# Layer 2's outer rows written from PSUM straight to interleaved columns, with inner and outer rows in output tiles of their own

## The chip, the cores and the metric

The kernel runs on one core of a Trainium2 chip. The metric is the time of one execution on the device, in microseconds (us). Before the change three runs took 1878.82, 1880.79 and 1884.20 us; the median is 1880.79. Engines are named as in the profile: PE is TensorE's matmul and PEld its weight load, DVE is VectorE, ACT is ScalarE, POOL is GpSimd and SP is SyncE. "L785" is line 785 of the kernel's file.

## The reference

Two layers of the same form work on x, which is (8 images, 32 channels, 252 x 252) in float32. Each layer normalizes its input by groups of two channels and adds a 5x5 convolution of that to it:

```python
def _gn(v, G=16, eps=1e-5):
    B_, C_, H_, W_ = v.shape
    g = v.reshape(B_, G, C_ // G, H_, W_)
    m = jnp.mean(g, axis=(2, 3, 4), keepdims=True)
    s = jnp.var(g, axis=(2, 3, 4), keepdims=True)
    return ((g - m) / jnp.sqrt(s + eps)).reshape(v.shape)
...
x = x + _L0_conv_ref(_gn(x), L0_conv_weight)
x = x + _L1_conv_ref(_gn(x), L1_conv_weight)
return x
```

The convolution pads by reflection (two pixels on each side) and is written with FFTs in the reference: `xp = jnp.pad(x, ..., mode='reflect')`, a product of transforms summed over the input channels, and the inverse transform without the border. Its output has the size of its input.

## The kernel before

**Layout.** A partition holds one channel of one of four phases: even or odd columns (`cp`) and even or odd rows (`rp`) of the image; `quad(cp, rp)` gives the 32 partitions of a phase, `halves[cp]` the 64 partitions of a column phase. On these phases the 5x5 convolution is a 3x3 convolution from 128 to 128 partitions. So a result tile has columns of one phase beside each other on a partition, and image rows need the two column phases interleaved again before they go out.

**Chunks.** An image is worked in 8 chunks of 16 phase rows (`NCH`, `ROWS`), a chunk as 4 tiles (`NT`) of 4 rows. Vertically a tile is computed by the polynomial method with six points: VectorE makes sums of input rows (`t24`, `t13`, `t05`), TensorE multiplies them with the weights of points 0 to 5, three column taps each (`product`, L685), and the products are put together. Rows 1 and 2 of each tile, the inner rows, need points 1 to 4 only. Rows 0 and 3, the outer rows, need point 0 and point 5 as well. In some chunks (`by_columns`) points 0 and 5 are treated by the same kind of method along the columns: VectorE makes sums and differences (`columns`, L618 to L628, into `sdiff` and `d`), TensorE multiplies four and four times at half length (`column_product`, L707, into `extra` and `sums`). The other chunks are called plain here.

**PSUM.** `m24` has points 2 and 4, `pairs13` points 1 and 3, `sums05` the two outer rows (bank e for row 0 or 3), `extra` the middle products of the column method. `sums05` is one tile for all chunks. VectorE writes into it what points 1 to 4 give to the outer rows (in plain chunks `parts05`, L763 and L764; in column chunks `column_parts`, L792 to L794), then TensorE adds the rest, then ScalarE reads it.

**Order.** All work stands in a table of due times, written by hand (`at`). The functions are called in the order of these times, and each engine executes its instructions in that order. A slot is 10.2 us long by the table, plus 5.1 us if the products of points 0 and 5 of a plain chunk stand in it, or 1.7 us for a column chunk. Chunks of layer 1 of image b+1 and of layer 2 of image b alternate (`order`); this document names a chunk by image, layer (0 for layer 1, 1 for layer 2) and number, as the code does: (3,1,4). For chunk i, `conv` is called with t0, t1 and t2, the starts of slots i, i+1 and i+2. In slot i are the products of points 1 to 4 and the inner rows. The products that complete the outer rows stand at the end of slot i+1. The outer rows are read at the start of slot i+2 (t2+0.05): by `outer` (L773, plain) or `outer_columns` (L785, columns), two ScalarE instructions each. They write into `y`, a tile of 16 rows.

**Layer 2's output.** In layer 2 `store` follows. `interleave` copies from y into an output tile `o` with every second column, for one of four groups of 4 rows and both column phases (L925): 8 copies of 64 partitions x 508 per chunk, at t2+0.7, +4.0, +6.5 and +8.5. An output tile holds 8 rows of the chunk (h is 0 or 1), and has buffers of its own pool, `opool`, of two. `send` issues the DMAs on SP's queue (L910), four per tile, at t2+5.3 and t2+9.8. The last chunk but one, (7,1,6), has its copies on VectorE and its DMAs on POOL's queue. In chunks (0,1,0) and (6,1,5) all is done in one slot (`m05`): there the outer rows come by VectorE (L771) from another tile. The last chunk, (7,1,7), is done in two halves (`store_half`).

**What stands around the read of sums05.** On ScalarE: before it the squares of layer 1 (L860) in some slots; after it two copies L925, then the seeds of `pairs13` (L729, L731), then the evacuation of `m24` (L737), `first_pair` (L744), and the seed of the middle products (L711). On VectorE: the write for the next chunk (L763 or L792) comes after points 0 and 5 (`points05`, L609) and before the sums of `columns`.

## Time and profile before

| | |
|---|---|
| three runs | 1878.82, 1880.79, 1884.20 us (median 1880.79) |
| the profiled execution | 1879.27 us, its span 1877.5 us |
| PE busy | 1839.2 us, 98% of the span |
| DVE busy | 1731.2 us, 92% |
| ACT busy | 1493.8 us, 80% |
| POOL busy | 396.2 us, 21% |
| ACT copies from y to o (L925) | 496 of 660 ns on average, 327.5 us |
| ACT reads of sums05 (L785, L773) | L785: 158, 94.5 us; L773 of 128x508: 45, 24.3 us |
| DMA | 369.07 MB, 197 GB/s on average |
| chain that ended last | 80% PE, 7% DVE, 6% DMA, 3% ACT |

How to read it: the span is the time from the first to the last instruction of the profiled execution, and the execution's own time is a little longer. A busy share is the time in which the engine had an instruction under way. A row of the groups gives line, engine, operation, output and input with their shapes, the number of instructions, then the busy time in us and the mean of one in ns, then the idle time of the engine just before them and what ended it. A row of the time line gives start and duration in us, and in brackets the idle time before it. A row of the waits gives the waiting instruction and whom it waited for, then us in total, the number of times and the longest. A row of the windows gives for a stretch of time the busy us of each engine with the number of instructions, then the granted clock of PE, the DMA share and GB/s.

### The profile page before, as it was taken

Reading aid. Unit: us, or ns where it says so; the run is one execution under the profiler, and the core shown is the slowest. Engines: PE = TensorE matmul, PEld = TensorE weight load, DVE = VectorE, ACT = ScalarE, POOL = GpSimd, SP = SyncE. Lnnn points to the kernel's source line nnn. Section 1 sums busy time; section 2 is a strip of 40 time slices with the busy share of each in tenths; the row PEclk is TensorE's granted clock in tenths of the full one; section 3 lists DMA queues with packets and bytes.
Section 4 is the critical chain, followed back from the end, with each engine's and each line's share of the span. In section 5 each row is a group of like instructions: output and inputs, shape, how many; then the busy total and the mean of one; then the engine's idle time right before and its main releaser. Section 6 shows DMA issues by size and latency. Waiting matters only on the chain.

```text
span 1877.5 us, 20381 instructions
## 1 busy us (share of the span) xinstructions
PE 1839.2 (98%) x5194; PEld 966.0 (51%) x5194; DVE 1731.2 (92%) x3030; ACT 1493.8 (80%) x2781; POOL 396.2 (21%) x855
## 2 busy tenths in 40 slices
PE   5999999999999999999999999999999999999998
PEld 4444455545555555555555455554555555555455
DVE  7988799999999999999999899999999999997796
ACT  5886788878887888888898798987898876765575
POOL 4543111131112211122111311113111141110211
PEclk8999999999999999999999999999999999999999
DMA  9877578878888877987878967888878866775785
GB/s 275 203 179 180 151 209 199 210 194 202 217 202 219 194 209 192 221 223 173 220 193 206 235 175 205 205 204 204 212 202 198 214 165 140 179 174 148 195 212 125
DMA packets 207110, 369.07 MB, mean 197 GB/s; under 512 B 19088, under 2 KB 173968, under 8 KB 196752
## 3 DMA queue, kind: packets, MB, share of 16 engines
q1 hardware_dynamic: 178832, 230.73, 49.8%
q0 software_dynamic: 27600, 134.20, 29.3%
q10 hardware_dynamic: 560, 2.83, 0.4%
q8 instruction: 41, 0.67, 0.2%
q14 instruction: 77, 0.63, 0.1%
HBM read 167.15 MB, written 67.39 MB: 125 GB/s over the span
## 4 chain that ended last, share of the span: by engine, by line
PE 80%; DVE 7%; DMA 6%; ACT 3%; issue 3%; SPq 0%; POOL 0%; DVEq 0%; ACTq 0%; POOLq 0%
PE m L685 28%; PE pairs L685 28%; PE sums L707 7%; PE extra L707 6%; PE sums L685 6%; PE extra L685 4%; DMA v<-y 2%; DMA st<-in_x_dram 1%; DMA v<-ytail 1%; DMA xs<-in_x_dram 1%; ACT o L925 1%; DVE sd L748 1%; DVE t L609 1%; DMA wraw<-in_L_conv_weight_dram 1%; DMA out_dram<-o 0%
## 5 line engine op out<-in xcount | busy, mean ns | idle before, releaser
L685 PE MATMUL pairs<-t,u 128*128 128x504 f32 (+2 forms) x1548 | 692.9, 586 | 5.4 <-ACT pairs L729 3.3
L685 PE MATMUL m<-t,u 128*128 128x508 f32 (+3 forms) x1560 | 674.8, 581 | 3.4 <-DVE u L526 1.9
L685 PEld LDWEIGHTS m<-t,u 128*128 128x128 f32 x1560 | 294.2, 189 | 317.1 <-issue 297.0
L685 PEld LDWEIGHTS pairs<-t,u 128*128 128x128 f32 x1548 | 290.2, 189 | 320.1 <-issue 289.1
L925 ACT COPY o<-y 64x508 f32<-64x508 f32 x496 | 327.5, 660 | 8.6
L748 DVE SCALAR_TENSOR_TENSOR sd<-sd,pairs 128x504 f32<-128x504 f32 (+2 forms) x258 | 164.2, 671 | 19.5 <-PE pairs L685 15.2
L707 PEld LDWEIGHTS extra<-sdiff,wc 128*128 128x128 f32 x680 | 125.9, 189 | 98.1 <-issue 47.8
L707 PE MATMUL extra<-sdiff,wc 128*128 128x252 f32 (+3 forms) x680 | 173.0, 376 | 3.4 <-ACT extra L711 2.3
L860 ACT ACTIVATE junk<-y,negk 128x1008 bf16<-128x1008 f32 (+1 forms) x144 | 147.4, 1024 | 31.1 <-PE extra L707 14.5
L557 POOL DMA_DIRECT2D v<-y x63 | 35.7, 567 | 622.7 <-DVE t L609 608.4
L737 ACT COPY sd<-m 128x504 f32<-128x504 f32 (+2 forms) x258 | 136.9, 581 | 33.3 <-DVE sums L794 28.1
L609 DVE SCALAR_TENSOR_TENSOR t<-v 128x1024 f32<-128x1024 f32 (+1 forms) x128 | 157.7, 1232 | 5.4 <-PE sums L685 5.4
L707 PE MATMUL sums<-d,u 128*128 128x252 f32 (+3 forms) x680 | 157.4, 374 | 0.0
L707 PEld LDWEIGHTS sums<-d,u 128*128 128x128 f32 x680 | 127.6, 189 | 24.9 <-issue 9.0
L685 PE MATMUL sums<-t,u 128*128 128x508 f32 (+5 forms) x312 | 133.6, 577 | 0.0
L567 DVE TENSOR_TENSOR v<-xs 128x1792 f32<-128x1792 f32 (+1 forms) x65 | 130.2, 2003 | 1.2
L241 ACT ACTIVATE st<-st,negk 128x1134 f32<-128x1134 f32 x98 | 121.7, 1242 | 3.2
L559 POOL DMA_DIRECT2D v<-y x63 | 54.3, 862 | 329.1 <-DMA v<-y 329.1
L159 ACT COPY xs<-xs 64x1792 f32<-64x1792 f32 (+2 forms) x97 | 109.3, 1129 | 13.4 <-POOL xs L151 11.1
L729 ACT ACTIVATE pairs<-m,means 128x504 f32<-128x504 f32 (+1 forms) x129 | 84.2, 653 | 44.5 <-PE m L685 36.0
L785 ACT ACTIVATE y<-sums 128x504 f32<-128x504 f32 (+1 forms) x158 | 94.5, 634 | 28.3 <-PE sums L707 19.2
L235 ACT ACTIVATE st<-st 128x1134 f32<-128x1134 f32 x98 | 112.5, 1148 | 5.0 <-DMA st<-in_x_dram 3.2
(174 smaller groups left out, 2529.7 us busy)
## 6 DMA issues: line engine op xcount, KB each, us to landing
v<-y POOLq DMA_DIRECT2D x63, 1032.0 KB, 6.1
st<-in_x_dram SPq DMA_DIRECT2D x111, 567.0 KB, 6.1
out_dram<-o SPq DMA_DIRECT2D x480, 126.0 KB, 5.9
v<-y POOLq DMA_DIRECT2D x63, 903.0 KB, 7.7
xs<-in_x_dram SPq DMA_DIRECT2D x96, 441.0 KB, 8.4
xs<-in_x_dram SPq DMA_DIRECT2D x44, 504.0 KB, 12.0
u<-ud SPq DMA_DIRECT2D x15, 1152.0 KB, 6.0
xs<-in_x_dram SPq DMA_DIRECT2D x16, 472.5 KB, 9.3
```

The lines of the kernel that those rows point to most:

```text
L159: copy(t[64:128, :, 0:256:2], t[0:64, :, 1:256:2])
L235: A.activation(junk, src, AF.Identity, accum_out=acc[:, 0, i : i + 1])
L241: A.activation(junk, src, AF.Square, bias=negk, accum_out=acc[:, 1, i : i + 1])
L567: (V.tensor_add if l else V.tensor_sub)(v[:, r0:r1], t[:, r0 + 2 : r1 + 2], t[:, r0:r1])
L609: stt(t, got["vt"][:, :, 0:2], 4.0 if l else -4.0, got["vt"][:, :, 2:4], ALU.mult, ALU.add)
L685: T.matmul(dst, u[:, k, 2 - i, :], rhs[:, j0 + i0 : j0 + i1, i : i + wo], start=(i == 0 and not add), stop=(i == 2), skip_group_check=add,)
L707: T.matmul(dst[:, 0, use], w, rhs[:, use], start=(i == 2), stop=True, skip_group_check=(i != 2))
L737: A.copy(got["sd"][:, 1 + e], m24[e][:, 0:n])
L748: stt(d, d, -2.0, pairs13[e][:, 0:n], ALU.mult, ALU.add)
L785: A.activation(y, src, AF.Copy, scale=1.0 - 2 * i, **total(3 * i))
L860: A.activation(dst, src, AF.Square, bias=negk, scale=1.0 if i else -1.0, accum_out=acc[:, 1, at_ : at_ + 1])
L925: copy(got["o", h][halves[s], 0:m, cp::2], got["y"][halves[cp], r : r + m, :])
```

## The change

In layer 2, chunks that are not done in one slot no longer copy their outer rows through y. `outer_out` reads a bank of sums05 on 64 partitions (one column phase) and writes it with every second column into an output tile: four instructions per chunk at t2+0.05, on ScalarE, where two on 128 partitions stood. For the column chunks the odd half of a bank now begins at column 256 of it (`half`), so that one instruction can read both halves; and the difference that was kept with the other sign is kept as it is (`columns`, `column_parts`), because a plain copy can't change a sign.

Output tiles now hold the outer rows (0 and 3 of all four tiles) or the inner rows (1 and 2), and not the first or second 8 rows. The inner rows are still copied from y, four copies per chunk at t2+4.0 and t2+6.5. The DMAs are again four per tile, now with every eighth image row; they stand at t2+3.3 for the outer tile and t2+9.8 for the inner one. An output tile is 256 columns wide, not 254.

For (7,1,6) the inner rows are copied by VectorE at t1+7.0, before the last outer products; of the outer rows row 0 is copied by ScalarE and row 3 by VectorE. The chunks (0,1,0) and (6,1,5) copy all from y as before, into the new tiles.

```diff
-                V.tensor_sub(d[:, :, :, 1, 0:mo], odd[:, :, :, 0:mo], t[:, :, :, 3 : 2 * mo + 2 : 2])
+                V.tensor_sub(d[:, :, :, 1, 0:mo], t[:, :, :, 3 : 2 * mo + 2 : 2], odd[:, :, :, 0:mo])
...
-            return tile_[:, e, i * nt * ne : i * nt * ne + nt * m].rearrange("p e (t w) -> p e t w", t=nt)
+            return tile_[:, e, i * nt * ne : (i + 1) * nt * ne].rearrange("p e (t w) -> p e t w", t=nt)[:, :, :, 0:m]
...
+        def outer_out(e: int, engines):
+
+            if e == 0:
+                got["outer"] = out_tile(b, c, "outer")
+            t = slice(*tiles(5 * e))
+            for cp, eng in enumerate(engines):
+                to, bank = got["outer"][halves[e]], sums05[halves[cp], e]
+                if columns:
+                    dst = to.rearrange("p t (j i a) -> p t i j a", i=2, a=2)[:, t, :, :, cp]
+                    src = bank[:, 0 : 2 * nt * ne].rearrange("p (i t j) -> p t i j", i=2, t=nt)[:, t]
+                else:
+                    dst, src = to[:, t, cp : 2 * wo : 2], rows(bank[:, 0:n])[:, t]
+                (eng.copy if eng is A else eng.tensor_copy)(dst, src)
...
-            V.tensor_sub(odd, m2[:, :, :, 0:no], odd)
-            V.tensor_sub(half(sums05, 1, both, no), odd, m12[:, :, :, 0:no])
+            if l:
+                V.tensor_sub(odd, odd, m2[:, :, :, 0:no])
+                V.tensor_add(half(sums05, 1, both, no), odd, m12[:, :, :, 0:no])
+            else:
+                V.tensor_sub(odd, m2[:, :, :, 0:no], odd)
+                V.tensor_sub(half(sums05, 1, both, no), odd, m12[:, :, :, 0:no])
...
-                at(t2 + 0.05, outer_columns, i)
+                if l == 0:
+                    at(t2 + 0.05, outer_columns, i)
+                else:
+                    at(t2 + 0.05, outer_out, i, (A, A))
...
-            at(t2 + 0.05, outer, 0)
-            at(t2 + 0.05, outer, 1)
+            for e in range(2):
+                if l == 0:
+                    at(t2 + 0.05, outer, e)
+                else:
+                    at(t2 + 0.05, outer_out, e, (V, V) if e and (b, c) == (B - 1, NCH - 2) else (A, A))
...
+    def out_tile(b: int, c: int, name: str):
+
+        pool, tag = (spool, "st") if last_but_one(b, c) else (opool, "o")
+        return pool.tile([P, NT, 2 * WOUT[1] + 2], F32, tag=tag, name=f"o_{name}_{b}_{c}")
+
+    def store(t1: float, t0: float, b: int, c: int, got, from_y: bool):
+
+        end = last_but_one(b, c)
+
+        def interleave(name: str, k: int):
+            if k == 0:
+                got[name] = out_tile(b, c, name)
+            i = 3 * k if name == "outer" else 1 + k
+            n = NT - 1 if (c, i) == (NCH - 1, 3) else NT
+            copy = V.tensor_copy if end else A.copy
             for cp in range(2):
-                copy(got["o", h][halves[s], 0:m, cp::2], got["y"][halves[cp], r : r + m, :])
...
+                copy(got[name][halves[k], 0:n, cp : 2 * WOUT[1] : 2], got["y"][halves[cp], i : 4 * n : 4, :])
+
+        def send(name: str):
+            for k in range(2):
+                for rp in range(2):
+                    r = 2 * (c * ROWS + (3 * k if name == "outer" else 1 + k)) - 1 + rp
+                    use = [j for j in range(NT) if 0 <= r + 8 * j < H]
+                    j, m, q = use[0], len(use), 2 * k + rp
+                    (G if end else S).dma_start(
+                        out[b, :, r + 8 * j : r + 8 * (j + m - 1) + 1 : 8, :],
+                        got[name][q * Q : (q + 1) * Q, j : j + m, 1 : 1 + W],
+                    )
+
+        if from_y:
+            for k, t in enumerate((0, 3.3)):
+                at(t0 + t, interleave, "outer", k)
+        for k, t in enumerate((t1 + 7.0, t1 + 7.2) if end else (t0 + 5.8, t0 + 7.8) if from_y else (t0 + 3.3, t0 + 5.8)):
+            at(t, interleave, "inner", k)
+        at(t0 + (4.6 if from_y else 2.6), send, "outer")
+        at(t1 + 7.3 if end else t0 + 9.1, send, "inner")
```

In the changed file `outer_out`'s copies are L778, those of the inner rows L958, the DMAs L966, and the write of column chunks into sums05 begins at L806.

## The prediction

> **What bounds the kernel now.** I read the page first (busy time, then the chain), then who TensorE waits for, then the time line of one pair of slots, then windows. Busy time and the windows:
>
> ```profile
> PE 1839.2 (98%) x5194; PEld 966.0 (51%) x5194; DVE 1731.2 (92%) x3030; ACT 1493.8 (80%) x2781; POOL 396.2 (21%) x855
> ```
> ```profile
> 890.00:964.00 74.00, 74.00 (x215) 40.50 (x214) 73.20 (x118) 66.28 (x117) 10.61 (x27) 1.00 0.84 207
> ```
>
> TensorE's matmuls follow each other without a hole, at the full granted clock, and in the 74 us from 890 to 964 VectorE is busy for 73.20 as well: two engines are full, ScalarE (66.28) is not. A change that relieves ScalarE is worth only the places where TensorE waits for ScalarE, and a wait put on VectorE is worth what of it gets through to TensorE. The table of TensorE's waits says how little there is to win:
>
> ```profile
> PE pairs L685 <- ACT pairs L729: 3.3, 4, 1.3
> PE extra L707 <- ACT extra L711: 2.3, 8, 0.8
> PE pairs L685 <- ACT pairs L731: 2.1, 1, 2.1
> ...
> PE extra L707 <- DVE sdiff L619: 0.5, 2, 0.3
> ```
>
> **The change, part by part. ScalarE's count.** Before, a layer-2 chunk has 2 copies PSUM to y (L773 or L785) and 8 copies y to o (L925). After, it has 4 from PSUM to o and 4 from y to o. For 61 chunks two instructions of about 0.66 us go: 61x2x0.66, some 80 us of ScalarE's 1493.8. Beside a full TensorE this is worth nothing by itself.
>
> **The wait that it adds.** The next chunk's first write into sums05 (L792, on VectorE; L806 after) waits for the last ScalarE read of that tile. That was two instructions on 128 partitions; it becomes four on 64, in the same place of ScalarE's order. What happens at that place, in the slot after a plain (not by_columns) layer-2 chunk has been closed:
>
> ```profile
> 888.36 1.23 DVE L609 SCALAR_TENSOR_TENSOR t<-v 128x1032 f32<-128x1032 f32 x1
> 888.59 1.08 ACT L773 ACTIVATE y<-sums 128x508 f32<-128x508 f32 x2 [2.13 <-PE sums L685]
> 889.70 1.34 ACT L925 COPY o<-y 64x508 f32<-64x508 f32 x2
> 889.70 0.69 DVE L792 TENSOR_TENSOR sums<-extra,sd 128x504 f32<-128x504 f32 x1
> ```
>
> ScalarE can't start before TensorE's last matmul (888.59), ends at 889.67, and VectorE starts at 889.70, 0.1 us later than it could. So whatever the four copies take over 1.08 us delays VectorE. Rows for a price:
>
> ```profile
> L925 ACT COPY o<-y 64x508 f32<-64x508 f32 x482 | 319.9, 664 | 8.4
> L773 ACT ACTIVATE y<-sums 128x508 f32<-128x508 f32 x45 | 24.3, 591 | 67.6 <-PE sums L685 67.6
> L785 ACT ACTIVATE y<-sums 128x512 f32<-128x512 f32 x38 | 24.0, 630 | 19.2 <-PE sums L707 19.2
> ```
>
> Two L773 take 1.08 us, so the second starts 0.49 after the first: 0.10 of overlap. Two L925 take 1.34: none. All of ScalarE's copies on 64 or 32 partitions in this trace follow each other without overlap (L867 on 32 partitions: four in 1.27 us at 0.308 each), so I take none. One copy: source and size of L773 (0.594), output stride of L785 (0.630): 0.61. Four with 0.01 between: 2.47 us. VectorE's write moves from 889.70 to 888.59+2.47+0.03 = 891.09: **1.37 us later** (ends kept for the range: as four L773 with overlap 3x0.49+0.594 = 2.06, so 0.98; as four L925 at 0.677 apart 2.70, so 1.60). *The Trainium skill ("ScalarE: Activation LUTs", section "What ACT_TABLE_LOAD costs") says that back-to-back activations overlap by about 93 ns; by that alone the four would take about 2.2 us, an estimate, and the sum below would be about 1.7 us lower. L925's 1.34 for two at 0.664 each speaks against it here.*
>
> **What is queued behind it on VectorE.** All of the next slots' work. From 889.70 to 964 VectorE waits for nobody (no row in its waits there), so the 1.37 us are not caught up. Who notices first:
>
> ```profile
> 963.93 0.68 DVE L619 TENSOR_TENSOR sdiff<-t 128x504 f32<-128x504 f32 x1
> ...
> 964.95 1.01 PE L707 MATMUL extra<-sdiff,wc 128*128 128x252 f32 x4
> ```
> ```profile
> 1079.54 0.68 DVE L619 TENSOR_TENSOR sdiff<-t 128x504 f32<-128x504 f32 x1
> ...
> 1080.27 1.01 PE L707 MATMUL extra<-sdiff,wc 128*128 128x189 f32 x4
> ```
>
> In the second, TensorE is late and starts 0.05 us after sdiff ends (1080.22). In the first it starts 0.34 after (964.61), so the margin is 0.29. It shrinks to this over five slots (chunk (b,0,2) 2.4, (b,0,3) 1.3, (b,0,4) 0.29), because VectorE has some 0.5 us more work per column slot than TensorE. So TensorE loses 1.37-0.29 = 1.08 us, 0.1 of it at (b,0,3) and the rest at (b,0,4). The same starting place and margin are found for images 1 to 6 (L792 at 439.35, 664.51, 889.70, 1115.64, 1341.19, 1566.85, each within 0.1 of L773's end; margins 0.27 to 0.29). **6 x 1.08 = +6.5 us** (ends 6x0.69 = 4.1 and 6x1.31 = 7.9).
>
> In the other slots VectorE mostly reaches the write later than the new end: after column chunks it comes 0.6 to 2.6 us behind ScalarE, and is itself 1.37 late where it is 0.6. After the second plain chunk of an image, (b,1,4), it comes 0.5 to 1.3 behind, so 0.1 to 0.9 is added, where the sdiff margins that follow are 1.1 to 1.9: nothing is lost. Image 0 has 1.9 to 2.8 there. The last image (from 1749) has holes of 1 to 2 us in VectorE's row every slot and sdiff margins of 2.9 and more: nothing.
>
> **What of it stays.** After the loss VectorE is still 0.29 behind its old place. At the end of an image TensorE stands for the mean's matmul (L346, 1043.32; its input ends at 1043.17), which comes that much later: 5 x 0.29 = 1.4 at most. In two of the five VectorE waited just before that for ScalarE (0.24 and 0.78 us), which now comes earlier. I take **+0.8** (0 to 1.4).
>
> **What ScalarE's relief gives.** Two L925 leave the queue in front of L711 in slot (b,1,7):
>
> ```profile
> 843.69 1.32 ACT L925 COPY o<-y 64x508 f32<-64x508 f32 x2
> ...
> 844.90 0.59 ACT L711 ACTIVATE extra<-extra 128x512 f32<-128x512 f32 x1
> ...
> 845.54 1.02 PE L707 MATMUL extra<-sdiff,wc 128*128 128x256 f32 x4 [0.23 <-ACT extra L711]
> ```
>
> TensorE's starts there are 0.4 us late five times and 0.9 once: 2.9 us. But one slot later, (b+1,0,0), sdiff arrives with no margin in four of six images (1080.27 above): what TensorE wins it waits there. I take **-0.4** (0 to -2.9).
>
> **The end.** Chunk (7,1,6) is copied by VectorE. Two of its eight copies stand in the last chunk's chain:
>
> ```profile
> 1867.50 0.33 DVE y L758
> ...
> 1867.86 0.42 DVE o L925
> ...
> 1868.29 0.43 DVE o L925
> ...
> 1868.74 0.42 DVE sd L763
> ```
>
> After, they run at about 1856, where VectorE stands idle (4.47 us before 1860.14). VectorE's last y comes 0.87 earlier (1869.15); ScalarE's four earlier copies end at 1869.58 instead of being waited past to 1870.06. **-0.5** (0 to -0.9). POOL's queue sends the inner tile some 3 us earlier, no one waits for it.
>
> **Edits at nothing.** The swapped operands (L628, L793, L794) are the same instructions; VectorE's order is unchanged. The odd half at column 256 makes 76 matmuls and 38 adds write 4x63 with a gap: the write of 252 takes 377 ns, of 256 379; at most 152 x 0.002 = 0.3 us, 0 taken. Output DMAs are the same 8 per chunk of rows of 1008 B, in the same order on SP; the first four are issued about 2 us earlier, behind ScalarE's outer copies. o's buffers are still written 13 us or more after the last send. Seeds (L729): four copies (2.47) stand before them where L773/L785 and two L925 (2.42 to 2.50) stood, and TensorE needs them 1.4 us later.
>
> **Sum.** 6.5+0.8-0.4-0.5 = **+6.4 us**. The profiled execution took 1879.27 (span 1877.5), 1.5 below the median of the runs, 1880.79. I add to the median: **1887.2**. Ends: 4.1+0-2.9-0.9 = +0.3 and 7.9+1.4 = +9.3.
>
> **Rivals.** (1) *Not slower: the wait does not reach TensorE.* It needs the four copies done within 1.08+0.29 = 1.37 us, 0.34 each, or VectorE's add waiting for half of them alone. Against it: no ScalarE copy of this size is under 0.49 apart, and L806 writes both banks at once. Then the relief and the end remain, -0.9 to -3.8: about 1879. (2) *Slower by more: the traffic.* The DMA share is 0.84 there, VectorE already waits 17.6 us for the accumulating loads (v<-y, 7 times, longest 3.5), and outputs now leave 2 us earlier, against them. Margins of TensorE to those loads are 2.7 us and more, which speaks against it; if seven waits grow by 1 us past that, +7 on top: 1894. (3) *Nothing happens*: both engines' changes are hidden, 1880.8; it needs what (1) needs, and goes with it.
>
> **How the numbers follow.** Forecast case 0.74, rival (1) with (3) 0.16, rival (2) 0.10. A measurement can tell about 0.3% (5.6 us) from no change. The forecast case reaches from +0.3 to +9.3 with 6.4 taken, so about 0.62 of it lies over +5.6; with rival (2) slower is 0.46+0.10 = 0.56. Faster needs all of the -3.8 and more: 0.02. The rest, 0.42, is the same. The range takes in rival (1)'s middle and the forecast's upper end with a part of rival (2): 1879 to 1891.5.
>
> **What would show it.** Right: in the slots at 439, 664, 890, 1115, 1341 and 1567 VectorE's first write to sums waits 1.4 us for the new ScalarE line, of which TensorE's wait for sdiff (L619) shows about 1 us per image, at (b,0,3) and (b,0,4); the copies follow each other every 0.62 us; L711 no longer holds TensorE; the last chunk's L758 is followed by L763 at once. Wrong: copies every 0.5 us (a third less loss); no wait for sdiff, which would mean that VectorE's lateness has an exit that I did not see; or waits on v<-y that were not there.

## The result, and the profile after the change

The changed kernel took **1912.46 us** (median of 4 runs, 1910.19 to 1912.64), the kernel before 1879.80 in the runs beside it (4 runs, 1875.82 to 1884.20): a ratio of **1.0170**, with a 95% interval of 1.0146 to 1.0195. It is slower by some 33 us. The prediction, 1887.2 (1879 to 1891.5), had the sign right and the size wrong by 25 us. The profiled execution of the changed kernel took 1912.64 us, its span 1910.9.

The lines that answer those shown of before, in the same order. First busy time, and the window of 74 us that starts at the same slot as the one shown of before (there 890 to 964, with PE 74.00 and DVE 73.20):

```profile
PE 1850.6 (97%) x5194; PEld 961.6 (50%) x5194; DVE 1736.1 (91%) x3028; ACT 1491.1 (78%) x2661; POOL 400.6 (21%) x855
```
```profile
905.50:979.50 74.00, 72.52 (x210) 39.14 (x209) 70.39 (x113) 64.96 (x108) 11.52 (x24) 1.00 0.80 202
```

ScalarE has 120 instructions fewer than before (2661, not 2781) and yet is busy for only 2.7 us less (1491.1, not 1493.8), where the prediction expected 80. TensorE now has holes (72.52 of 74), and VectorE, which was full, has larger ones (70.39). The group of the new copies tells why ScalarE won nothing. This is the table of groups with shapes kept apart; the figure after the bar is the sum in us, then the mean of one copy in ns:

```profile
L778 ACT COPY o_outer<-sums 64x512 f32<-64x512 f32 x140 | 152.9, 1092 | 22.8 <-PE sums L707 21.2
...
L778 ACT COPY o_outer<-sums 64x508 f32<-64x508 f32 x88 | 54.4, 618 | 79.9 <-PE sums L685 78.8
```

A plain chunk's copy (64x508) takes 0.618 us, as priced (0.61). A column chunk's copy (64x512), of nearly the same size, takes **1.092**. What that does in the slots, from the time line (start, duration). Slot (3,1,1) stands behind a plain chunk, slot (3,1,2) behind a column chunk:

```profile
903.58 1.23 DVE L609 SCALAR_TENSOR_TENSOR t<-v 128x1032 f32<-128x1032 f32 x1
904.14 2.51 ACT L778 COPY o_outer<-sums 64x508 f32<-64x508 f32 x4 [2.37 <-PE sums L685]
906.68 0.69 DVE L806 TENSOR_TENSOR sums<-extra,sd 128x504 f32<-128x504 f32 x1 [1.88 <-PE m L685]
```
```profile
931.79 4.40 ACT L778 COPY o_outer<-sums 64x512 f32<-64x512 f32 x4
936.22 0.66 ACT L729 ACTIVATE pairs<-m,means 128x508 f32<-128x508 f32 x1
936.23 0.69 DVE L806 TENSOR_TENSOR sums<-extra,sd 128x504 f32<-128x504 f32 x1 [1.22 <-ACT o_outer L778]
...
936.93 3.67 PE L685 MATMUL pairs<-t,u 128*128 128x508 f32 x8 [0.49 <-ACT pairs L729]
```
```profile
953.94 0.68 DVE L619 TENSOR_TENSOR sdiff<-t 128x504 f32<-128x504 f32 x1
...
954.67 1.12 PE L707 MATMUL extra<-sdiff,wc 128*128 128x252 f32 x4 [0.47 <-DVE sdiff L619]
```

Behind the plain chunk four copies take 2.51 us (priced at 2.47). Behind the column chunk they take 4.40. Two things wait for them. The seed L729, which ScalarE writes into `pairs` before TensorE adds to it, starts 4.43 us after the first copy, and TensorE waits for it. In the same slot before, it started 2.53 us after L785 and ended 1.3 us before TensorE's matmuls on `pairs`:

```profile
916.24 1.14 ACT L785 ACTIVATE y<-sums 128x512 f32<-128x512 f32 x2
...
918.77 0.66 ACT L729 ACTIVATE pairs<-m,means 128x508 f32<-128x508 f32 x1
...
920.72 3.57 PE L685 MATMUL pairs<-t,u 128*128 128x508 f32 x8
```

VectorE's write L806 waits too, and hands its lateness on to the next sdiff (L619), for which TensorE waits at 954.67. The table of waits sums it up (us in total, times, longest):

```profile
DVE sums L806 <- ACT o_outer L778: 27.4, 34, 2.2
...
PE pairs L685 <- ACT pairs L729: 18.1, 27, 3.0
...
PE extra L707 <- DVE sdiff L619: 6.6, 14, 0.5
```

Before, TensorE waited 3.3 us for L729 and 0.5 for sdiff. Slot by slot (first matmul of one slot to the first of the next), from slot (2,1,0) to (3,1,0): five slots behind a column chunk of layer 2 are 0.74 to 0.80 us longer than before, two slots of layer 1, (3,0,3) and (3,0,4), 0.74 each, (3,0,7) with the mean's matmuls 0.63; (2,1,7) is 0.5 shorter and (4,0,0) 0.25 longer. The sum is +5.7, and the image took 231.0 us instead of 225.2.

Two smaller places that the prediction named are as it said. L711 no longer holds TensorE in slot (b,1,7), and in the last chunk L763 follows L758 at once:

```profile
858.85 0.58 ACT L711 ACTIVATE extra<-extra 128x512 f32<-128x512 f32 x1
...
860.15 0.92 PE L707 MATMUL extra<-sdiff,wc 128*128 128x256 f32 x4
```
```profile
1904.08 0.41 DVE L758 SCALAR_TENSOR_TENSOR y<-sd 128x254 f32<-128x254 f32 x1
...
1904.40 0.42 DVE L763 TENSOR_TENSOR sd<-pairs,sd 128x254 f32<-128x254 f32 x1
```

### The profile page after: what moved, and what is told of

It is laid out like the page before. It is cut to its first block, busy times and chain, and to the rows that moved or that the text cites. A ratio compares the mean times of both kernels' runs of the same rounds, so it can differ in the third digit from the quotient of the medians.

```text
span 1910.9 us, 20250 instructions
## 1 busy us (share of the span) xinstructions
PE 1850.6 (97%) x5194; PEld 961.6 (50%) x5194; DVE 1736.1 (91%) x3028; ACT 1491.1 (78%) x2661; POOL 400.6 (21%) x855
## 4 chain that ended last, share of the span: by engine, by line
PE 63%; DVE 13%; ACT 12%; issue 5%; DMA 2%; ACTq 0%; SPq 0%; DVEq 0%; POOL 0%
PE pairs L685 24%; PE m L685 19%; PE sums L685 6%; ACT o_outer L778 6%; PE sums L707 5%; PE extra L707 5%; PE extra L685 4%; DVE sd L748 1%; DMA out_dram<-o_inner 1%; ACT pairs L729 1%; ACT st L235 1%; DVE d L622 1%; DVE t L602 1%; DMA out_dram<-o_outer 1%; ACT junk L884 1%
## 5 line engine op out<-in xcount | busy, mean ns | idle before, releaser
L685 PE MATMUL pairs<-t,u 128*128 128x504 f32 (+2 forms) x1548 | 696.6, 588 | 23.6 <-ACT pairs L729 18.1
L778 ACT COPY o_outer<-sums 64x512 f32<-64x512 f32 (+1 forms) x242 | 218.6, 903 | 102.9 <-PE sums L685 78.8
L958 ACT COPY o_inner<-y 64x508 f32<-64x508 f32 x248 | 165.4, 667 | 6.4 <-DMA out_dram<-o_inner 2.6
L148 POOL COPY xs<-xs 64x4 f32<-64x4 f32 (+3 forms) x113 | 51.3, 454 | 378.8 <-DMA xs<-in_x_dram 282.2
L729 ACT ACTIVATE pairs<-m,means 128x504 f32<-128x504 f32 (+1 forms) x129 | 84.2, 653 | 50.4 <-PE m L685 46.5
```

The costliest lines, as they stand in the source:

```text
L685: T.matmul(dst, u[:, k, 2 - i, :], rhs[:, j0 + i0 : j0 + i1, i : i + wo], start=(i == 0 and not add), stop=(i == 2), skip_group_check=add,)
L729: A.activation(dst, src, AF.Identity, bias=norm[b, l][1][:, 0:1])
L778: (eng.copy if eng is A else eng.tensor_copy)(dst, src)
L958: copy(got[name][halves[k], 0:n, cp : 2 * WOUT[1] : 2], got["y"][halves[cp], i : 4 * n : 4, :])
```

## The experiments

**Theories.** The two shapes of L778 differ in how they go through the output. In a plain chunk neighbouring elements land 2 elements apart, 8 bytes. In a column chunk the pattern is "t i j": all even-half columns of a row first, then all odd-half ones, so neighbours land 4 elements apart, 16 bytes. Theory A: this distance makes the copy 1.10 us, and the length of the copies is the whole loss. Rival C: it is the source (two halves of a bank) or the pattern of one dimension more. Rival D: the new output tiles, their DMAs of every eighth row or the earlier sends cost time. Theory E is about the way in which the copies cost: not through the late seed alone, but through VectorE's wait as well.

For each kernel three figures are compared: the median with its ratio to the kernel before, run on the same chip; the time per image in the profiled execution, from the first matmul of slot (1,1,0) to that of (6,1,0), divided by 5; and the end, from TensorE's last matmul to the end of the span.

| kernel | median us | ratio (95%) | per image us | end us |
|---|---|---|---|---|
| before | 1878.4 to 1880.0 | 1 | 225.5 | 8.8 |
| changed | 1912.46 | 1.0170 (1.0146 to 1.0195) | 231.0 | 5.5 |
| other order | 1879.95 | 1.0007 (0.9998 to 1.0017) | 226.3 | 5.5 |
| 8 bytes, plain source | 1878.69 | 1.0007 (0.9998 to 1.0017) | 226.3 | 5.6 |
| tiles only | 1876.82 | 0.9991 (0.9980 to 1.0003) | 225.6 | 5.5 |
| columns only, other order | 1879.42 | 1.0003 (0.9993 to 1.0013) | 226.4 | 5.6 |
| plain only | 1884.78 | 1.0037 (1.0022 to 1.0052) | 227.8 | 5.5 |
| changed, seed between | 1940.01 | 1.0313 (1.0297 to 1.0329) | 235.6 | 5.7 |
| chunks 5 to 7 only, other order | 1872.81 | 0.9968 (0.9957 to 0.9980) | 225.1 | 5.5 |
| before, end on SP | 1874.67 | 0.9981 (0.9969 to 0.9992) | 225.3 | 5.7 |

**1. The other order of the same copy.**

```diff
-                    dst = to.rearrange("p t (j i a) -> p t i j a", i=2, a=2)[:, t, :, :, cp]
-                    src = bank[:, 0 : 2 * nt * ne].rearrange("p (i t j) -> p t i j", i=2, t=nt)[:, t]
+                    dst = to.rearrange("p t (j i a) -> p t j i a", i=2, a=2)[:, t, :, :, cp]
+                    src = bank[:, 0 : 2 * nt * ne].rearrange("p (i t j) -> p t j i", i=2, t=nt)[:, t]
```

> The computation is unchanged: only the order of elements within one column-chunk copy of the outer rows (L778) is another, row, then column pair, then even/odd, so that consecutive elements land 8 bytes apart instead of 16, while the PSUM source now jumps between the two halves of its bank (1 KB apart) at every element. Theory A (the 16-byte output stride is what makes this copy 1.10 us instead of the 0.61 that was predicted): the copy falls to 0.62 us, four take 2.5 us instead of 4.4, TensorE's waits for the seed L729 fall from 18 us to 4 or so and the time to 1880 to 1892. Theory C (the order of the source, or a pattern of one dimension more, is what is slow): the copy stays at 1.1 us or gets slower, and the time is 1910 or more. If the copy falls and the time stays above 1900, neither is the cause of the time.

The group of the same copies in this kernel, and its table of waits:

```profile
L778 ACT COPY o_outer<-sums 64x512 f32<-64x512 f32 x140 | 87.7, 626 | 23.9 <-PE sums L707 22.3
```
```profile
PE extra L707 <- DVE sdiff L619: 4.8, 7, 0.7
...
PE pairs L685 <- ACT pairs L729: 3.2, 4, 1.3
DVE sums L806 <- ACT o_outer L778: 2.7, 5, 1.3
```

The copy fell from 1.092 to 0.626 us, ScalarE's busy time to 1429.4 us (64 below before), the wait for L729 to 3.2 and the time by some 31 us (the ratio from 1.0170 to 1.0007), to that of the kernel before. One order of two nested loops made the whole loss. Theory A holds; C's jumping source costs nothing.

**2. The same distance with the source as it was.**

```diff
-                    dst = to.rearrange("p t (j i a) -> p t i j a", i=2, a=2)[:, t, :, :, cp]
+                    dst = to.rearrange("p t (i j a) -> p t i j a", i=2, a=2)[:, t, :, :, cp]
```

> Leaves out the interleaving of even and odd columns: in column chunks the outer rows are copied in the order of the changed kernel's source (the even half, then the odd half of each row) to output elements 8 bytes apart, so the two halves of a row lie side by side in the output instead of interleaved. Source as in the changed kernel, output stride as in the plain chunks. Theory A: the copy takes 0.62 us and the time is that of the kernel with the other order within 4 us, 1880 to 1892. Theory C: the copy stays at 1.1 us, and the time at 1912. If this one falls to 0.62 and the other order does not, then the jumping source is slow as well.

626 ns again, and the same ratio. So it is the output, not the source.

**3. The tiles and the DMAs alone.** Column chunks go back to `outer_columns` (with scale 1 for both halves in layer 2), plain ones to `outer`, and the outer tile is filled from y. Only (7,1,6) stays direct.

```diff
-                if l == 0:
+                if True:
                     at(t2 + 0.05, outer_columns, i)
...
-                if l == 0:
+                if l == 0 or (b, c) != (B - 1, NCH - 2):
                     at(t2 + 0.05, outer, e)
...
-            store(t1, t1 + 1.5 if m05 else t2 + 0.7, b, c, got, m05 is not None)
+            store(t1, t1 + 1.5 if m05 else t2 + 0.7, b, c, got, (b, c) != (B - 1, NCH - 2))
```

> The part with the tiles alone: outer rows go through y again (two copies on 128 partitions in the place behind TensorE's last matmul, as before), but inner and outer rows keep output tiles of their own, with output DMAs of every eighth row; only the last chunk but one keeps the direct copies. Theory A (all of the loss comes from the column copies): 1878 to 1883, no difference from before. Theory D (the new tiles, the wider row distance of the DMAs or the earlier sends cost something): 1888 or more, up to 1912 if all of the loss is theirs. In both ScalarE is as busy as before, near 1494 us.

No loss, 225.6 us per image. Of rival D, the wider rows and the other tiles fall: they cost nothing here. The earlier sends are not in this kernel, whose DMAs stand at t2+5.3 and t2+9.8 as before; they are in the kernel of experiment 1, which is no slower than before, and there as in the changed kernel VectorE waits less for the loads `v<-y` than before (17.6 us before, 5.5 in the changed kernel). The median is 1.7 us under before, within the interval; the end alone is 3.3 us shorter (experiment 9).

**4. and 5. Which way the copies cost.** The first try put the copies of column chunks behind the seed.

```diff
-                    at(t2 + 0.05, outer_out, i, (A, A))
+                    at(t2 + 2.62, outer_out, i, (A, A))
```

> The changed kernel with one order changed: in column chunks the four copies L778 stand behind the seed L729 of the next slot on ScalarE instead of ahead of it. The copies stay at 1.10 us. If what costs is the seed (TensorE's group L685 waits for it, 18 us as the waits give it and 28 us between starts): those waits fall to about 4 us, and the time falls by 15 to 25 us, to 1888 to 1898, although VectorE's first write L806 now comes another 0.6 us later. If what costs is VectorE's wait at L806 (theory E): nothing is won, VectorE is late by 0.6 us more in each of 36 slots, and the time is 1912 to 1930, with TensorE's waits for sdiff L619 above the 6.6 us of the changed kernel.

This gave 2071.74 us (ratio 1.1035) and answers nothing. At that place the copies stand behind VectorE's next write L806 in the order, so they read the next chunk's sums, and ScalarE waits for VectorE (62.8 us in all for L812) where VectorE should have waited for ScalarE: another program. The second try keeps the order on all other engines and puts the seed between the second and the third copy.

```diff
-                    at(t0 + step * (i + h / 3) + (0.85 if columns and i == 3 and h else 0.0), product, k, h)
+                    at(t0 + step * (i + h / 3 * (1.0 if i or nt < NT else 0.85)) + (0.85 if columns and i == 3 and h else 0.0), product, k, h)
...
-            at(t, seed, e)
+            at(t if e or first or nt < NT else t0 + 1.46, seed, e)
...
-                    at(t2 + 0.05, outer_out, i, (A, A))
+                    at(t2 + (1.47 if i else 0.05), outer_out, i, (A, A))
```

> The changed kernel with its copies of 1.10 us, and only ScalarE's order changed: in column chunks the seed L729 of the next slot stands between the second and the third of the four copies instead of behind the fourth. The order on all other engines is the same. The seed is then in time (ScalarE is free at 2.2 us into the slot, when TensorE's matmuls for it end at about 2.6), and VectorE's first write L806 comes about 0.9 us later (behind 2.2 + 0.9 + 2.2 us of ScalarE instead of 4.4). If only the late seed costs time: TensorE's waits for L729 fall from 18 us to about 4 and the time to 1888 to 1895. If VectorE's lateness costs as well (theory E): VectorE has no time to catch up, TensorE's waits go over to sdiff (L619, 6.6 us in the changed kernel) and the time does not fall, 1910 to 1940.

The time line of this kernel in a slot behind a column chunk, and its waits:

```profile
944.48 2.21 ACT L778 COPY o_outer<-sums 64x512 f32<-64x512 f32 x2
946.72 0.66 ACT L729 ACTIVATE pairs<-m,means 128x508 f32<-128x508 f32 x1
947.40 2.15 ACT L778 COPY o_outer<-sums 64x512 f32<-64x512 f32 x2
948.95 3.74 PE L685 MATMUL pairs<-t,u 128*128 128x508 f32 x8
949.59 0.69 DVE L806 TENSOR_TENSOR sums<-extra,sd 128x504 f32<-128x504 f32 x1 [1.90 <-ACT o_outer L778]
...
952.83 1.13 PE L707 MATMUL extra<-sdiff,wc 128*128 128x256 f32 x4
```
```profile
DVE sums L806 <- ACT o_outer L778: 55.7, 40, 3.2
...
PE extra L707 <- DVE sdiff L619: 14.0, 19, 0.9
...
PE pairs L685 <- ACT pairs L729: 3.9, 3, 3.0
```

The seed is in time now (its waits 18.1 to 3.9 us), L806 comes 5.11 us after the first copy instead of 4.44, and the time rose by some 27 us, to 1940. 0.67 us in each of the 38 slots behind a column chunk is 25. So about all of VectorE's added lateness reaches TensorE, at sdiff (14.0 us instead of 6.6) and at the mean's matmul L346 (10.2 us for VectorE instead of 1.0). Theory E holds in this sense: in the changed kernel the late seed is where TensorE's waiting shows most, but a seed that is in time at VectorE's cost wins nothing. What an early seed would give if VectorE were held no longer than in the changed kernel was not run.

**6. and 7. The parts alone.** The kernel columns_ji copies only column chunks directly, in the order of experiment 1; plain_only only plain ones.

```diff
-                if l == 0:
+                if l == 0 or (b, c) != (B - 1, NCH - 2):
                     at(t2 + 0.05, outer, e)
...
-            store(t1, t1 + 1.5 if m05 else t2 + 0.7, b, c, got, m05 is not None)
+            store(t1, t1 + 1.5 if m05 else t2 + 0.7, b, c, got, m05 is not None or not columns and (b, c) != (B - 1, NCH - 2))
```

> Direct copies from PSUM in column chunks alone, in the order with 8 bytes between elements; the outer rows of plain chunks go through y again (two copies on 128 partitions behind TensorE's last matmul), the last chunk but one excepted. The theory that the step of the prediction on plain chunks is right (after a plain chunk VectorE's first write waits for four copies of 0.62 us in place of two, and TensorE waits for sdiff at the chunk (b,0,4) about 0.9 us in each of six images, as seen in the kernel with the other order): these waits go, and the time is 3 to 5 us under that kernel's, 1875 to 1877. The rival that four copies instead of two cost after column chunks too: the waits at (b,0,4) stay above 0.5 us, and the time stays at 1879 to 1881.

```diff
-                if l == 0:
+                if True:
                     at(t2 + 0.05, outer_columns, i)
...
-            store(t1, t1 + 1.5 if m05 else t2 + 0.7, b, c, got, m05 is not None)
+            store(t1, t1 + 1.5 if m05 else t2 + 0.7, b, c, got, m05 is not None or columns)
```

> The reverse: direct copies in plain chunks alone, as in the changed kernel; the outer rows of column chunks go through y again. If the loss of the plain chunks is what the prediction said, TensorE waits for sdiff at (b,0,4) about 0.9 us in six images, and the time is 1879 to 1882, 3 to 5 us over the kernel that copies only column chunks directly, and none of the 32 us that the changed kernel lost to the 16-byte stride is here. If plain chunks cost nothing: 1875 to 1877. If the 32 us came from plain chunks as well: above 1890.

Neither came as the theory had it. Column chunks alone took 1879.42, no less than both together, as the rival said. The slot (3,0,4) is still 0.67 us longer than before (1.0 with both kinds): VectorE's write now waits for the four copies behind the first column chunk instead, as the time line of columns_ji in slot (2,1,2) shows.

```profile
690.36 2.52 ACT L778 COPY o_outer<-sums 64x512 f32<-64x512 f32 x4
692.91 0.66 ACT L729 ACTIVATE pairs<-m,means 128x508 f32<-128x508 f32 x1
692.92 0.69 DVE L806 TENSOR_TENSOR sums<-extra,sd 128x504 f32<-128x504 f32 x1 [0.75 <-ACT o_outer L778]
```

With both kinds direct VectorE is already late by 1.4 us there, and waits for nothing; alone, each kind makes it late. The two costs do not add, they stand in for each other. What is won at (3,0,4) goes elsewhere: this kernel lacks the relief in front of L711, for which TensorE waits 3.3 us (0.5 with both kinds direct, 2.3 before). Plain chunks alone took 1884.78, 0.37% more than before and 3 us over the upper end expected. In its profiled execution the slots (3,0,3) and (3,0,4) are 0.2 and 0.6 us longer and (2,1,3) 0.4, a sum of 1.2; beyond that (b+1,0,0) is 1.7 and 1.3 us longer in two of the five images, (3,0,0) and (7,0,0). The trace shows the chain there: at the end of these two images, and of no other, VectorE waits for the load `v<-ytail` (3.1 and 2.5 us), and TensorE then 1.2 us for sdiff in that slot. Such late loads are in the kernel before too (four, up to 2.8 us), so a part of this loss may be chance; what makes the load late is not shown. The relief in (b,1,7) is there in four of the five images (0.4 to 0.5 us), so its lack is not the reason.

**8. Direct copies where they help (late_ji).** From these runs: the loss is made in slots (b,1,0) to (b+1,0,4), the relief of L711 in (b,1,7). So only chunks 5, 6 and 7 are copied directly, in the order of experiment 1.

```diff
-                if l == 0:
+                if l == 0 or c < 5:
                     at(t2 + 0.05, outer_columns, i)
...
-                if l == 0:
+                if l == 0 or c < 5:
                     at(t2 + 0.05, outer, e)
...
-            store(t1, t1 + 1.5 if m05 else t2 + 0.7, b, c, got, m05 is not None)
+            store(t1, t1 + 1.5 if m05 else t2 + 0.7, b, c, got, m05 is not None or c < 5)
```

> Direct copies (8 bytes between elements) in the chunks 5, 6 and 7 of an image alone; the outer rows of chunks 0 to 4 go through y again. Theory: VectorE's added wait reaches TensorE at (b,0,4) through the chunks (b,1,0) to (b,1,3), while the relief of ScalarE in front of L711 in the slot (b,1,7) comes from the chunks behind them. Then the waits for sdiff at (b,0,4) (0.9 us in each of six images with all chunks direct) are gone, those for L711 (0.4 us five times, 0.9 once in the kernel before) as well, the end stays 3 us shorter, and the time is 3 to 5 us under the kernel before: a ratio of 0.997 to 0.9985. The rival that what TensorE wins at one place it loses at the next, because VectorE is as full as TensorE: the ratio is 0.9985 to 1.001.

```profile
880.00:954.00 74.00, 74.00 (x215) 40.41 (x214) 73.19 (x120) 65.78 (x118) 10.25 (x24) 1.00 0.77 202
```

This window of late_ji starts near the slot of the windows above. TensorE is full again; in the whole execution VectorE waits 0.5 us for L778 at L806, and TensorE 0.3 for sdiff and 0.5 for L711. The time is 1872.81, a ratio of 0.9968 (0.9957 to 0.9980): **faster than both kernels**, by 6.0 us (3.8 to 8.1) against before. The profiled executions are 8.4 us apart: 3.3 at the end, 2.1 in the five images and the rest ahead of slot (1,1,0). The end needs no direct copy (experiment 9), so the direct copies themselves are worth less than the 6.0: against the kernel of experiment 9, run beside it, late_ji's median is 1.9 us lower (1872.81 and 1874.67), and the runs of the two overlap (1870.83 to 1877.92, 1872.38 to 1879.96).

**9. What made the end 3 us shorter.** The end was shorter by 3.1 to 3.3 us in every kernel with the new `store`, though ScalarE's last copy ended only 0.5 earlier behind TensorE's last matmul. The records of the last line before and after show it (duration in ns: least, median, longest; then first and last start):

```profile
L1132 POOLq DRAIN  x3: 34/102/7252, 1869.5 to 1877.2; - x3
```
```profile
L1174 POOLq DRAIN  x3: 34/102/7250, 1899.1 to 1910.6; - x3
```

POOL drains for 7.25 us behind its last DMA. Before, this starts at 1869.46 and sets the end at 1877.5; after, it starts 6.2 us ahead of TensorE's last matmul and is over in time. The test is the kernel before with its last four DMAs of chunk (7,1,6) on SP:

```diff
-                send_rows(b, c, h, s, got, (G, G) if end else (S, S))
+                send_rows(b, c, h, s, got, (G, G) if end and h == 0 else (S, S))
```

> The kernel before, with one edit: the second four output DMAs of the last chunk but one leave on SP's queue instead of POOL's. In the kernel before POOL issues its last DMA at 1869.5 us, then stands in a drain of 7.25 us until 1876.7, and the program ends 0.8 us later; in the changed kernel the same drain of 7.25 us starts 9 us earlier and is over when the other queues end. If the drain sets the end: POOL's drain starts at about 1866 and ends at 1873.5, SP's last DMAs set the end, and from TensorE's last matmul to the end it is 6 to 7.5 us instead of 8.8; the time falls by 1 to 3 us. If the drain only waits for the end of all else: the 8.8 us stay.

The end fell from 8.8 to 5.7 us, the time by 3.6 us (ratio 0.9981, 0.9969 to 0.9992), both by a little more than expected. The drain set the end.

**10. and 11. What the distance costs.** Two kernels copied at other distances, for the durations alone (one execution each, 1901.07 and 1881.35 us).

```diff
+                if columns and c in (1, 2, 3, 5):
+                    s = {1: 1, 2: 3, 3: 4, 5: 8}[c]
+                    x, j = {1: (1, 128), 3: (3, 42), 4: (2, 64), 8: (4, 32)}[s]
+                    if s in (1, 3):
+                        dst = to[:, :, x * j * cp + s // 3 : x * j * (cp + 1) + s // 3].rearrange("p t (j x) -> p t x j", x=x)
+                    else:
+                        dst = to.rearrange("p t (j x a) -> p t x j a", x=x, a=2)[:, :, :, :, cp]
+                    src = bank[:, 0 : 4 * x * j].rearrange("p (t x j) -> p t x j", t=4, x=x)
```

> Leaves out the right placement of the outer rows in column chunks 1, 2, 3 and 5: the same 512 (504 at 12 bytes) elements per partition are copied from consecutive places of PSUM to elements that lie 4, 12, 16 and 32 bytes apart in the output tile, one distance for each chunk number; chunk 7 and the plain chunks are as in the changed kernel. What one copy takes says what the rule is. Theory A1 (a cost per distance, growing): 0.59, 0.85, 1.10, 1.9 us or so. Theory A2 (a step: once neighbours lie 16 bytes or more apart, each element costs the same): 0.6, 0.6 or 1.1, 1.1, 1.1. Theory C (the order of the source is what costs): 0.6 everywhere, since the source is consecutive here.

The time line of this kernel, four copies a row, chunks 1 (4 bytes), 2 (12 bytes), 3 (16) and 5 (32):

```profile
925.78 2.35 ACT L786 COPY o_outer<-sums 64x512 f32<-64x512 f32 x4
...
953.18 3.49 ACT L786 COPY o_outer<-sums 64x504 f32<-64x504 f32 x4
...
981.41 4.41 ACT L786 COPY o_outer<-sums 64x512 f32<-64x512 f32 x4
...
1038.28 4.38 ACT L786 COPY o_outer<-sums 64x512 f32<-64x512 f32 x4
```

Shown is image 3. One copy, as the median of its kind: 0.58 us at 4 bytes, 0.63 at 8 (experiment 2), 0.86 at 12, 1.10 at 16 and 1.09 at 32. Neither A1 nor A2 alone: little up to 8 bytes, half of the way at 12, all at 16, and nothing more behind that. The Trainium skill says of this, in "SBUF — State Buffer", section "Specifications (TRN2)", that SBUF works in lines of 16 bytes and that at least two accesses must fall into a line for the full rate. At 8 bytes two elements share a line, at 16 none do, at 12 only some: the five rows fit this rule. The page gives no size for the penalty; here it is 0.47 us for 512 elements.

```diff
+                if columns and c in (1, 2):
+                    x = 4 if c == 1 else 2
+                    dst = to.rearrange("p t (x j a) -> p t x j a", x=x, a=2)[:, :, :, :, cp]
+                    src = bank[:, 0:512].rearrange("p (t j x) -> p t x j", t=4, x=x)
+                if eng is V:
+                    dst = to[:, 0:4, 1:253].rearrange("p t (j x a) -> p t x j a", x=2, a=2)[:, :, :, :, cp]
+                    src = rows(bank[:, 0:n])[:, :, 0:126].rearrange("p t (x j) -> p t x j", x=2)
...
+                if name == "inner" and c in (3, 6):
+                    dst = got[name][halves[k], 0:n, 1:253].rearrange("p t (j x a) -> p t x j a", x=2, a=2)[:, :, :, :, cp]
+                    src = src[:, :, 0:126].rearrange("p t (x j) -> p t x j", x=2)
```

> The kernel with the other order, with some copies that leave out the right placement. Outer rows of column chunks 1: the PSUM source is read with 16 bytes between elements, the output written with 8. Chunks 2: source with 8 bytes, output with 8. Inner rows (source y in SBUF) of chunks 3 and 6: output written with 16 bytes between elements, 504 per partition. In the last chunk but one the same with VectorE's copies, from SBUF and from PSUM. If it is the writing alone that costs (two elements' time each at 16 bytes and more): chunks 1 and 2 take 0.62 us, the inner copies of chunks 3 and 6 about 1.12 instead of 0.667. If reading at a distance costs as well: chunks 1 at 1.1 us. For VectorE: 0.42 us (before, at 8 bytes) becomes 0.8 or more if its writes follow the same rule, and stays at 0.42 if the rule is ScalarE's.

The groups, shapes apart (all L785 64x512 write at 8 bytes and read PSUM at 8 bytes, at 16 or in jumps of 1 KB; L969 64x508 writes at 8, the 64x504 rows at 16):

```profile
L969 ACT COPY o_inner<-y 64x508 f32<-64x508 f32 x188 | 125.5, 668 | 5.9 <-DMA out_dram<-o_inner 3.3
L785 ACT COPY o_outer<-sums 64x512 f32<-64x512 f32 x140 | 87.6, 626 | 23.5 <-PE sums L707 21.9
...
L969 ACT COPY o_inner<-y 64x504 f32<-64x504 f32 x60 | 67.5, 1125 | 1.1
...
L969 DVE COPY o_inner<-y 64x504 f32<-64x504 f32 x4 | 2.5, 624 | 0.1
...
L785 DVE COPY o_outer<-sums 64x504 f32<-64x504 f32 x2 | 2.1, 1062 | 2.2 <-ACT o_outer L785 2.2
```

Reading PSUM at 8 or 16 bytes costs nothing (chunk 1, at 16: 0.63 us). Writing SBUF at 16 bytes costs ScalarE the same from SBUF (0.668 to 1.125). VectorE pays too: 0.422 to 0.624 from SBUF and 0.688 to 1.062 from PSUM, compared with its copies at 8 bytes in experiment 1's kernel:

```profile
L958 DVE COPY o_inner<-y 64x508 f32<-64x508 f32 x4 | 1.7, 422 | 0.1
...
L778 DVE COPY o_outer<-sums 64x508 f32<-64x508 f32 x2 | 1.4, 688 | 3.0 <-ACT o_outer L778 3.0
```

## Why the prediction was wrong, point by point

- **The step that failed: "One copy: source and size of L773 (0.594), output stride of L785 (0.630): 0.61. Four with 0.01 between: 2.47 us"**, with 2.06 to 2.70 as ends. It took one price for both kinds of chunk. For plain chunks it holds (0.618, four in 2.51). For column chunks, 38 of the 61, one took 1.09 and four 4.40. The distance at which such a copy writes stood in the diff ("p t i j a": j runs innermost, 4 elements apart); it was not read, and the rows used as bounds, L773, L785 and L925, all write at 4 or 8 bytes. Experiment 1 alone, which changes nothing but the order of the loops in this copy, moves the time from 1912.5 to 1880; experiment 2 shows that it is the output's distance.
- **"Seeds (L729): four copies (2.47) stand before them where ... (2.42 to 2.50) stood"** followed from that price and fell with it: 4.43 us stand before them, TensorE needs them about 0.7 us sooner, and five slots per image are 0.74 to 0.80 us longer. This is 3.9 of the 5.7 us per image.
- **"... after column chunks it comes 0.6 to 2.6 us behind ScalarE, and is itself 1.37 late where it is 0.6"**, so that nothing is lost there, holds with copies of 0.62 us, because VectorE is already late by the plain chunk's wait (experiment 1, and the slot of 6 and 7 that shows each cost alone). With 4.40 us it fails: L806 waits 1.2 us in (b,1,2), and the slots (b+1,0,3) and (b+1,0,4) lose 0.74 each. Experiment 5 shows how little of such a wait VectorE can swallow.
- **The wait behind plain chunks, +6.5, was right.** It can be read where nothing else disturbs, in the kernel of experiment 1. L806 came 2.55 us behind the first copy instead of 1.11: 1.44 later (predicted 1.37). TensorE's waits are at (b,0,3) and (b,0,4) as said, and the slots (4,0,3) and (4,0,4) are 0.18 and 0.99 longer: 1.17 per image (predicted 1.08).

```profile
887.46 2.52 ACT L778 COPY o_outer<-sums 64x508 f32<-64x508 f32 x4 [2.14 <-PE sums L685]
...
890.01 0.69 DVE L806 TENSOR_TENSOR sums<-extra,sd 128x504 f32<-128x504 f32 x1 [1.50 <-PE m L685]
```
```profile
964.16 0.68 DVE L619 TENSOR_TENSOR sdiff<-t 128x504 f32<-128x504 f32 x1
...
964.89 1.12 PE L707 MATMUL extra<-sdiff,wc 128*128 128x252 f32 x4 [0.72 <-DVE sdiff L619]
```

- **No overlap of copies on 64 partitions** was right: four take 2.51 us at 0.618 each. The Trainium skill ("ScalarE: Activation LUTs", section "What ACT_TABLE_LOAD costs") gives an overlap of about 93 ns for activations back to back; it does not show in these copies.
- **The residual at the mean, +0.8, and L711's relief, -0.4:** in experiment 1 the mean's matmul waits no longer than before (1.5 us in all, from start to start), so the +0.8 did not come; slot (b,1,7) is 0.5 shorter in all five images, and (b+1,0,0) 0.25 longer in two of them, so that a part of the relief is given back one slot later, as said. With the wait behind plain chunks, 4.2 us were measured there in the five images (0.84 each) and 1.2 from slot (6,1,0) to TensorE's last matmul: 5.4, against 6.9 predicted (6.5+0.8-0.4).
- **The end, -0.5 (0 to -0.9), was too small.** What it named was there (from TensorE's last matmul to ScalarE's last copy 1.7 us instead of 2.15). But "POOL's queue sends the inner tile some 3 us earlier, no one waits for it" was wrong: the program's end waits for POOL's drain, and the end is 3.3 us shorter.
- **ScalarE's count, -80 us**, would have been -64 with the right order and was -2.7. That this is worth nothing by itself was right: with 64 us less of ScalarE's work the time is the same as before.
- **The rivals.** (1), that the wait does not reach TensorE, is refuted. (2) priced the traffic at +7; experiment 3 shows no cost of tiles and of DMAs of wider rows, and VectorE's waits for `v<-y`, which were to grow, fell. (3) did not happen. None of them doubted the duration of the new copy.

With the copy at its predicted price the change gives +1.4 us (-0.4 to +3.2), which is less than the +6.4 of the prediction; 2.8 us of the difference are the end.

## What to carry to other kernels

Price a strided copy by the distance at which its innermost loop writes, read from the pattern in the code, and take a row with that distance; if there is none, the upper end is open. When the loops of a copy can be nested either way, let the output run in the tighter one, and the jumps be read from PSUM. And a wait put in front of a full engine is paid nearly whole, so a change that adds one belongs only where that engine has room: here in three of the eight chunks, where the kernel became 0.3% faster, over half of it by the end, and in the others not.

## What was not expected of the hardware

- Writing float32 to SBUF at 16 bytes or more between neighbours takes 1.09 to 1.13 us for 504 or 512 elements on ScalarE instead of 0.58 to 0.67; VectorE pays in the same way. Reading PSUM at 16 bytes, or jumping by 1 KB at each element, costs nothing on ScalarE.
- POOL's drain behind its last DMA takes 7.25 us in twelve kernels and 7.85 in one. Before, it ended the program; in the changed kernel the last DMA on POOL's queue leaves early enough, and the drain is over 4.5 us before the end.
- After a wait TensorE may work at a lower granted clock for a while. In the changed kernel it is busy for 3.0 of the 6 us from 190 to 196, and then does 7 matmuls in 4 us, at a clock of 0.57. In the kernel of experiment 1 it is busy for 4.7 of those 6 us, and then does 11 in 4 us at 1.00. The windows of the two from 196 to 200 follow; the wait just before them is 3.0 us long in the first and 1.3 in the second. Waits of 2.1 us near 178 were followed by such a stretch in some kernels (the kernel before: 0.69 from 180 to 184) and not in others (that of experiment 9, the same program up to its last chunks: 1.00); what decides that is not shown, and it is not the change.

```profile
196.00:200.00 4.00, 4.00 (x7) 1.64 (x6) 3.76 (x9) 2.14 (x5) 0.00 (x0) 0.57 0.01 2
```
```profile
196.00:200.00 4.00, 4.00 (x11) 1.86 (x10) 3.62 (x9) 3.63 (x12) 0.00 (x0) 1.00 0.00 0
```
